# A selective scan of 64 states: every fourth state's input scaled on GpSimd token-major and turned by TensorE, one scan instruction a state

## The chip, the cores and the metric

The kernel runs on one core of one Trainium2 chip. The metric is the device time of one execution in microseconds; the kernel before takes 7624.67 us, the median of three runs (7620.87 to 7626.77). The engines are named as in the profile: PE is TensorE (PEld its weight loads), DVE is VectorE, ACT is ScalarE, POOL is GpSimd, SP is SyncE, which issues the DMAs.

## The reference

Four conditional layers follow one another on x of shape (16, 256, 256): an adapter, a bidirectional selective state-space layer with an MLP, and two transformer layers. Only the second layer's scan is touched, and it is where most instructions are. Cut to that:

```python
def _ssm(h, in_w, xproj_w, dt_bias, A_log, Dskip, out_w):   # h: (16, 256, 256)
    xz = h @ in_w
    xs, z = jnp.split(xz, 2, axis=-1)                        # 512 channels each
    xs = jax.nn.silu(xs)
    proj = xs @ xproj_w
    dt = jax.nn.softplus(proj[..., :D_INNER] + dt_bias)
    Bm = proj[..., D_INNER:D_INNER + D_STATE]                # 64 states
    Cm = proj[..., D_INNER + D_STATE:]
    A = -jnp.exp(A_log)
    def step(hst, ins):
        dt_t, B_t, C_t, x_t = ins
        dA = jnp.exp(dt_t[:, :, None] * A)
        hst = hst * dA + (dt_t * x_t)[:, :, None] * B_t[:, None, :]
        y_t = jnp.einsum('bds,bs->bd', hst, C_t)
        return (hst, y_t)
    ...                                                      # scan over 256 tokens
    y = jnp.swapaxes(ys, 0, 1) + xs * Dskip
    return y * jax.nn.silu(z) @ out_w
h_fwd = _ssm(h, ...)
h_bwd = jnp.flip(_ssm(jnp.flip(h, 1), ...), 1)
x = x + gate * (h_fwd + h_bwd)
```

## The kernel before

**Units and states.** A unit is one batch row in one direction: 16 x 2 = 32 units, each with 64 states; `steps` is the list of all 2048 (unit, state) pairs. For one state all 512 channels and 256 tokens are worked at once, channel-major: 128 partitions, four channel groups (`IC` = 4) of 256 tokens, 1024 elements a partition. A block below is eight consecutive states.

**What one state costs, in the order of the data.** `drive` (L931) makes the input on GpSimd: `dtx` (dt times x) times the state's row of B, which a DMA has spread over all partitions (`load_b`, four states at a time, SBUF tile `bb`). `decay` (L946) makes exp(dt x A) on ScalarE, four instructions a state, into PSUM. Three one-bank tiles `decays` take half a state (two channel groups) each in turn; column 0 of each group stays zero, so that one instruction can run through two groups without carrying a value over. `scan` (L974) runs two scans of 512 elements on VectorE, decay from PSUM, input from SBUF, result in place of the input in `h`; in the backward direction it walks the tokens from the end. Then `h` is multiplied by the state's row of C: for five states of eight on VectorE (L977), with C spread over the partitions by two TensorE transposes into the PSUM bank `cs` (`spread`, L961); for three of eight on GpSimd (L981), with C spread by a DMA (`load_c`, SBUF tile `cb`). `add_up` (L992) turns `h` by eight transposes that add into the PSUM tile `y`, which collects all 64 states.

**Order.** The main loop runs over k. In its turn k it emits the input of state k + 4 (`AHEAD`), the scan and C multiply of k, the decays of k + 1 and the sum of k - 2 (`BEHIND`), then one piece of the side work: `front` and `back` of the neighbouring units and `rest`, which is all other layers of a batch row. A scheduler orders each engine's instructions from this, by its own view of what is ready; GpSimd's multiplies are held in the order in which they are emitted (`keep_in_program_order`). Each engine works its queue in order. `h` tiles come from a ring of `NH` = 11. All DMAs are issued by SyncE, in one queue: `bb` and `cb` as well as the weights of all layers. Once a unit, `front` ends with four GpSimd multiplies of the same size (L452 to L461), the last of which makes `dtx`.

**PSUM.** Eight banks: three `decays`, one `cs`, two for `y`, two in `ps_g`, which the side work shares. After the last scan, the side work of the last batch row also takes the four banks of `decays` and `cs` (list `alone`).

Of the kernel before, what the change touches and what calls it, by code (L numbers as in the profile page):

```python
# [22 lines left out]
NS = 64  # L23
EPS = 1e-5


# [28 lines left out]
def kernel(ctx: ExitStack, tc: tile.TileContext, a: dict, out: bass.AP):  # L55
# [68 lines left out]
    SG = 4  # L124
    ND = 3
    NH = 11
    res = ctx.enter_context(tc.tile_pool(name="res", bufs=1))
# [6 lines left out]
    ps_y = ctx.enter_context(tc.tile_pool(name="ps_y", bufs=1, space=PSUM))  # L134
    ps_c = ctx.enter_context(tc.tile_pool(name="ps_c", bufs=1, space=PSUM))
    ps_g = ctx.enter_context(tc.tile_pool(name="ps_g", bufs=2, space=PSUM))
# [119 lines left out]
    for d in ("fwd", "bwd"):  # L256
        an = res.tile([P, IC, NS], F32, name=f"a_neg_{d}")
        nc.sync.dma_start(an, a[f"L1_cond_{d}_A_log"].rearrange("(c p) s -> p c s", p=P))
        nc.scalar.activation(an, an, AF.Exp)
        nc.vector.tensor_scalar(an, an, -1.0, None, ALU.mult)  # L260
        a_neg.append(an)
        w_bc.append(res.tile([P, IC, 2 * NS], F32, name=f"w_bc_{d}"))
        nc.sync.dma_start(w_bc[-1], chunked(a[f"L1_cond_{d}_xproj_w"])[:, :, DI:])
        w_out.append(res.tile([P, IC, D], F32, name=f"w_out_{d}"))
        nc.sync.dma_start(w_out[-1], chunked(a[f"L1_cond_{d}_out_w"]))


    decays = [ps_y.tile([P, 2, T], F32, name=f"decay{j}") for j in range(ND)]
    for dc in decays:
        nc.vector.memset(dc[:, :, 0:1], 0.0)  # L270

# [101 lines left out]
    def front(u):  # L373
# [13 lines left out]
        w_in, w_dt = wfront.pop(u)  # L387
        xz = s2.tile([P, 2 * IC, T], F32, name="xz")
        for m in range(0, 2 * IC, 2):
            px = halves(bank1("pxz"))  # L390
            for j in range(2):
                for c in range(DC):
                    nc.tensor.matmul(  # L393
                        px[:, j], w_in[:, c, (m + j) * P : (m + j + 1) * P], hT[:, c],
                        start=(c == 0), stop=(c == DC - 1),
                    )
                yield
            nc.scalar.copy(xz[:, m : m + 2], px)
        nc.scalar.activation(xz, xz, AF.Silu)
        exp_table()  # L400
        yield
        pb = bank1("pbc")
        for c in range(IC):
            nc.tensor.matmul(pb[:, :T], w_bc[d][:, c], xz[:, c], start=(c == 0), stop=(c == IC - 1))
        bc = s1.tile([P, T], F32, name="bc", tag="uu")
# [3 lines left out]
        yield  # L409
        pt = bank1("pct")  # L410
        for t in range(NT):
            nc.tensor.transpose(pt[:, t * P : (t + 1) * P], bc[:, t * P : (t + 1) * P], ident)
        cT = s2.tile([P, NT, NS], F32, name="cT")
        nc.scalar.copy(cT, pt[:, :T].rearrange("p (t s) -> p t s", t=NT)[:, :, NS:])
        yield


        pr = s1.tile([P, IC, T], F32, name="pr")
        for m in range(0, IC, 2):
            pp = halves(bank1("pdt"))  # L420
            for j in range(2):
                for c in range(IC):
                    nc.tensor.matmul(  # L423
                        pp[:, j], w_dt[:, c, (m + j) * P : (m + j + 1) * P], xz[:, c],
                        start=(c == 0), stop=(c == IC - 1),
                    )
                yield
            for j in range(2):
                nc.scalar.activation(  # L429
                    pr[:, m + j], pp[:, j], AF.Identity, bias=col(f"L1_cond_{name}_dt_bias", m + j)  # L430
                )
            yield
# [27 lines left out]
        yield  # L460
        tc.keep_in_program_order(nc.gpsimd.tensor_tensor(dtx, dt, xz[:, 0:IC], ALU.mult))  # L461
        st[u] = (xz, cT, bd, dt, dtx)
        yield

    def back(u, yg):
# [12 lines left out]
        for m in range(DC):  # L478
            xb = xs[b][:, m]
            nc.vector.scalar_tensor_tensor(  # L480
                xb, po[:, m], m_mamba[:, 4 + m, b : b + 1], xb, ALU.mult, ALU.add
            )
# [81 lines left out]
    def heads2(q, k, v, o, rows):  # L564

        exs, exTs = {}, {}
        for i in range(16 + 3):
# [30 lines left out]
            if i % 2 and i >= 3:  # L598
                yield
                po = bank2("po")[:, :T]  # L600
                for h in (i - 3, i - 2):
                    exT = exTs.pop(h)
                    base = (h % 2) * 64
                    for kt in range(NT):
                        nc.tensor.matmul(  # L605
                            po[base : base + 64], v[:, kt, h * 64 : (h + 1) * 64], exT[:, kt],
                            start=(kt == 0), stop=(kt == NT - 1),
                        )
# [55 lines left out]
    def heads3(q, k, v, oT):  # L664
# [28 lines left out]
        def values(g):  # L693
# [14 lines left out]
            po = bank2("po3")[:, :T]  # L708
            for j in range(4):
                for kt in range(NT):  # L710
                    nc.tensor.matmul(
# [180 lines left out]

    bbs, cbs, ys, made, hs, skips = {}, {}, {}, {}, {}, {}
    cs = ps_c.tile([P, 2, T], F32, name="cs")
    steps = [(u, s) for u in range(len(units)) for s in range(NS)]
    turn = [0]

    def load_b(u, g):
        bd = st[u][2]
        bb = s3.tile([P, SG, T], F32, name="bb")  # L900
        nc.sync.dma_start(bb, bd[g * SG : (g + 1) * SG, :].partition_broadcast(P))
        bbs[u, g] = bb

    def load_c(u, g):
        bd = st[u][2]
        cb = s3.tile([P, 3, T], F32, name="cb")
        nc.sync.dma_start(
            cb,
            bd[NS + 8 * g + 1 : NS + 8 * g + 8 : 3, :].partition_broadcast(P),
        )  # L910
        cbs[u, g] = cb

    def drive(k):
        u, s = steps[k]
        if s % SG == 0:
            if s == 0:
                load_b(u, 0)
            if s + SG < NS:
                load_b(u, s // SG + 1)
            if s % 8 == 0:  # L920
                load_c(u, s // 8)
        if s == 0:
# [4 lines left out]
            skips[u] = skip  # L927
        h = s3.tile([P, IC, T], F32, name="h", bufs=NH)
        bb = bbs[u, s // SG][:, s % SG]
        tc.keep_in_program_order(  # L930
            nc.gpsimd.tensor_tensor(h, st[u][4], bb.unsqueeze(1).to_broadcast([P, IC, T]), ALU.mult)  # L931
        )
        hs[k] = h

    def decay(k):
        u, s = steps[k]
        d = units[u][1]

        when = slice(1, T) if d == 0 else slice(T - 2, None, -1)
        made[k] = []  # L940
        for i in range(2):
            dc = decays[turn[0] % ND]
            turn[0] += 1
            for j in range(2):
                c = 2 * i + (j if d == 0 else 1 - j)
                nc.scalar.activation(  # L946
                    dc[:, j, 1:T], st[u][3][:, c, when], AF.Exp, scale=a_neg[d][:, c, s : s + 1]
                )
            made[k].append(dc)


    near = [k for k, (u, s) in enumerate(steps) if s % 8 in (0, 2, 3, 5, 6)]
    nth = {k: i for i, k in enumerate(near)}

    def spread(i):

        if i >= len(near):
            return
        u, s = steps[near[i]]
        for t in range(NT):  # L960
            nc.tensor.transpose(  # L961
                cs[:, i % 2, t * P : (t + 1) * P], st[u][1][:, t, s : s + 1].to_broadcast([P, P]), ident
            )

    def scan(k):
        u, s = steps[k]
        d = units[u][1]
        h = hs[k]
        for i, dc in enumerate(made.pop(k)):
            hv = h[:, 2 * i : 2 * i + 2].rearrange("p c t -> p (c t)")  # L970
            dv = dc.rearrange("p c t -> p (c t)")
            if d == 1:
                hv = hv[:, ::-1]
            nc.vector.tensor_tensor_scan(hv, dv, hv, 0.0, ALU.mult, ALU.add)  # L974
        if k in nth:
            c = cs[:, nth[k] % 2]
            nc.vector.tensor_tensor(h, h, c.unsqueeze(1).to_broadcast([P, IC, T]), ALU.mult)  # L977
        else:
            c = cbs[u, s // 8][:, (s % 8) // 3]
            tc.keep_in_program_order(  # L980
                nc.gpsimd.tensor_tensor(h, h, c.unsqueeze(1).to_broadcast([P, IC, T]), ALU.mult)  # L981
            )

    def add_up(k):
# [4 lines left out]
        for n, h in enumerate(([skips.pop(u)] if s == 0 else []) + [hs.pop(k)]):  # L989
            for t in range(NT):  # L990
                for c in range(IC):
# [5 lines left out]
                    )  # L997

# [138 lines left out]
    for k in range(AHEAD):  # L1139
        drive(k)  # L1140
    decay(0)
    spread(0)
    spread(1)
    other = late()
    for k in range(len(steps) + BEHIND):
        if k < len(steps):
# [6 lines left out]
            if k + 1 < len(steps):  # L1153
                decay(k + 1)
        if k >= BEHIND:
            add_up(k - BEHIND)
        if k - 1 in nth:
            spread(nth[k - 1] + 2)
        if k >= BEHIND:
            u, s = steps[k - BEHIND]  # L1160
            if s == NS - 1:
# [5 lines left out]
                for i in range(2):  # L1167
                    py = halves(bank1("py"))
                    for j in range(2):
# [3 lines left out]
                    nc.vector.tensor_tensor(  # L1173
                        yg[:, 2 * i : 2 * i + 2], py, st[u][0][:, IC + 2 * i : IC + 2 * i + 2], ALU.mult
                    )
# [6 lines left out]
    drain(other)  # L1182
    alone += [None] + [t.rearrange("p c t -> p (c t)") for t in (decays[0], cs, decays[1])]
    alone += [None, decays[2].rearrange("p c t -> p (c t)")]
    while waiting:
# [29 lines left out]
```

## Time and profile before

| | |
|---|---|
| median of three runs | 7624.67 us |
| span of the profiled execution | 7616.3 us |
| GpSimd input multiply, L931, x2048 | 4793.5 us busy, 2367 ns each |
| VectorE scan of 512, L974, x4096 | 4748.8 us busy, 1213 ns each |
| TensorE sums, L992, x16384 | 2385.3 us busy |
| ScalarE decays, L946, x8192 | 3641.4 us busy, 471 to 474 ns each |
| GpSimd C multiply, L981, x768 | 1813.2 us busy, 2361 ns each |
| VectorE C multiply, L977, x1280 | 1533.5 us busy, 1215 ns each |
| TensorE spreads of C, L961, x2560 | 521.6 us busy |
| DMA | 675.90 MB, mean 89 GB/s |

In the groups of instructions a line names the source line, engine and operation, then output and inputs with their partitions x elements and how many there are; after the first bar stand the busy time of the group and the mean of one in ns, after the second the time the engine sat idle just before them and what ended it. A wait line names who waited for whom, the total, how often and the longest. A timeline line has start, length, engine and instruction; neighbours of one kind are merged.

### The profile page before, as it was taken

The numbers are of one execution on the slowest core, as the hardware profiler recorded it, in microseconds if no ns is written. First come the engines' busy times: TensorE is split into PE (matmuls) and PEld (weight loads), VectorE is DVE, ScalarE is ACT, GpSimd is POOL, SyncE is SP. The second block draws the span as 40 slices with busy tenths as digits, with TensorE's granted clock in tenths as the row PEclk, the third lists the DMA queues.
The fourth block names the chain that finished last, engine by engine and source line by source line (L and its number), as shares of the span: only waits on it lengthen the run. The fifth ranks groups of instructions, "written<-read, shape, count | busy, mean of one in ns | idle before, by whom it ended". The sixth has DMA issues, their size and how long they took to land.

```text
span 7616.3 us, 100847 instructions
## 1 busy us (share of the span) xinstructions
PE 6249.2 (82%) x35471; PEld 4952.4 (65%) x35471; DVE 6860.6 (90%) x6887; ACT 5431.2 (71%) x12141; POOL 6843.8 (90%) x2959
## 2 busy tenths in 40 slices
PE   7568888888888888888888888888888888888778
PEld 4456676666667666676666666666666766666655
DVE  3988999999999999999999999999999999999982
ACT  4567777777777777777777777777777777777753
POOL 3999999999999999999999999999999999999960
PEclk8679999999999999999999999999999999999999
DMA  4112232222322222232222223222232222322221
GB/s 166 54 65 92 89 102 76 87 92 88 103 85 93 80 91 95 92 103 73 88 92 91 100 86 98 78 92 93 87 106 79 94 84 89 101 91 89 73 68 49
DMA packets 331644, 675.90 MB, mean 89 GB/s; under 512 B 24724, under 2 KB 204032, under 8 KB 326784
## 3 DMA queue, kind: packets, MB, share of 16 engines
q1 hardware_dynamic: 331136, 669.44, 26.7%
q8 instruction: 280, 4.59, 0.2%
q14 instruction: 228, 1.87, 0.1%
HBM read 650.22 MB, written 10.75 MB: 87 GB/s over the span
## 4 chain that ended last, share of the span: by engine, by line
DVE 47%; POOL 15%; issue 14%; ACT 12%; PE 10%; DVEq 0%; POOLq 0%; ACTq 0%
DVE h L974 34%; POOL h L931 8%; DVE h L977 8%; ACT decay L946 5%; POOL h L981 5%; PE y L992 3%; DVE maxima L682 1%; ACT L155 1%; PE dense L500 1%; PE down L511 1%; PE bank L108 1%; PE po L605 1%; POOL uu L452 1%; POOL dt L458 1%; POOL dtx L461 1%
## 5 line engine op out<-in xcount | busy, mean ns | idle before, releaser
L974 DVE TENSOR_TENSOR_SCAN h<-decay,h 128x512 f32<-128x512 f32 x4096 | 4748.8, 1213 | 283.1 <-ACT decay L946 196.6
L931 POOL TENSOR_TENSOR h<-dtx,bb 128x1024 f32<-128x1024 f32 x2048 | 4793.5, 2367 | 129.2 <-PE y L992 128.4
L992 PE MATMUL y<-ident,h 128*128 128x128 f32 x16384 | 2385.3, 292 | 693.0 <-POOL h L981 639.1
L992 PEld LDWEIGHTS y<-ident,h 128*128 128x128 f32 x16384 | 2054.6, 151 | 1047.6 <-POOL h L981 733.1
L946 ACT ACTIVATE decay<-dt,a_neg_bwd 128x255 f32<-128x255 f32 x4096 | 1816.8, 471 | 759.9 <-DVE h L974 718.3
L946 ACT ACTIVATE decay<-dt,a_neg_fwd 128x255 f32<-128x255 f32 x4096 | 1824.6, 474 | 613.0 <-DVE h L974 571.6
L981 POOL TENSOR_TENSOR h<-h,cb 128x1024 f32<-128x1024 f32 x768 | 1813.2, 2361 | 289.8 <-DVE h L974 275.1
L977 DVE TENSOR_TENSOR h<-h,cs 128x1024 f32<-128x1024 f32 x1280 | 1533.5, 1215 | 66.2 <-PE cs L961 56.6
L961 PE MATMUL cs<-ident,cT 128*128 128x128 f32 x2560 | 521.6, 294 | 131.8 <-DVE h L977 130.3
L961 PEld LDWEIGHTS cs<-ident,cT 128*128 128x128 f32 x2560 | 331.4, 147 | 216.0 <-DVE h L977 192.0
L572 PE MATMUL sc<-k,q 64*128 64x256 f32 x960 | 293.4, 429 | 16.7 <-ACT ex L581 16.0
L393 PE MATMUL pxz<-hTm,w_in 128*128 128x256 f32 x1024 | 267.6, 388 | 15.9 <-DVE maxima L682 12.1
L679 PE MATMUL sc<-kd,qk 128*128 128x512 f32 x490 | 251.4, 614 | 33.5 <-DVE maxima L682 20.8
L700 PE MATMUL scT<-qk,kd 128*128 128x256 f32 x984 | 251.1, 386 | 28.7 <-DVE qk L691 23.2
L581 ACT ACTIVATE ex<-sc,nmax 128x256 f32<-128x256 f32 x480 | 222.7, 468 | 71.2 <-DVE nmax L577 68.5
L423 PE MATMUL pdt<-xz,w_dt 128*128 128x256 f32 x1024 | 247.3, 385 | 0.0
L572 PEld LDWEIGHTS sc<-k,q 64*128 64x128 f32 x960 | 172.6, 200 | 105.3 <-issue 34.2
L393 PEld LDWEIGHTS pxz<-hTm,w_in 128*128 128x128 f32 x1024 | 181.4, 194 | 53.1 <-DVE maxima L682 15.5
L700 PEld LDWEIGHTS scT<-qk,kd 128*128 128x128 f32 x984 | 175.5, 190 | 60.7 <-ACT pr L429 25.0
L577 DVE TENSOR_REDUCE nmax<-sc 128x2 f32<-128x512 f32 x240 | 163.9, 683 | 49.5 <-PE sc L572 48.8
L423 PEld LDWEIGHTS pdt<-xz,w_dt 128*128 128x128 f32 x1024 | 190.7, 194 | 22.2
L595 ACT COPY exT<-pt 128x512 f32<-128x512 f32 x240 | 140.0, 583 | 86.2 <-PE pt L591 84.0
(350 smaller groups left out, 7571.4 us busy)
## 6 DMA issues: line engine op xcount, KB each, us to landing
bb<-bd SPq DMA_DIRECT2D x512, 512.0 KB
cb<-bd SPq DMA_DIRECT2D x256, 384.0 KB
l2w<-in_L_cond_W_dram SPq DMA_DIRECT2D x32, 1024.0 KB
l3w<-in_L_cond_W_dram SPq DMA_DIRECT2D x32, 1024.0 KB
l1w<-in_L_cond_mlp_w_dram SPq DMA_DIRECT2D x48, 512.0 KB
w_in<-in_L_cond_fwd_in_w_dram SPq DMA_DIRECT2D x16, 1024.0 KB
w_dt<-_L_cond_fwd_xproj_w_dram SPq DMA_DIRECT2D x16, 1024.0 KB
w_in<-in_L_cond_bwd_in_w_dram SPq DMA_DIRECT2D x16, 1024.0 KB
```

The lines of the kernel that those rows point to most:

```text
L393: nc.tensor.matmul(px[:, j], w_in[:, c, (m + j) * P : (m + j + 1) * P], hT[:, c], start=(c == 0), stop=(c == DC - 1),)
L423: nc.tensor.matmul(pp[:, j], w_dt[:, c, (m + j) * P : (m + j + 1) * P], xz[:, c], start=(c == 0), stop=(c == IC - 1),)
L572: nc.tensor.matmul(sc[:, t], q[base : base + 64, ch, t * P : (t + 1) * P], k[base : base + 64, ch], start=True, stop=True,)
L679: nc.tensor.matmul(sc, q[:, g, t * P : (t + 1) * P], kd[g % 2][:, 2 * i : 2 * i + 2], start=True, stop=True)
L700: nc.tensor.matmul(sc[:, kt], kd[g % 2][:, j, kt * P : (kt + 1) * P], q[:, g], start=True, stop=True)
L931: nc.gpsimd.tensor_tensor(h, st[u][4], bb.unsqueeze(1).to_broadcast([P, IC, T]), ALU.mult)
L946: nc.scalar.activation(dc[:, j, 1:T], st[u][3][:, c, when], AF.Exp, scale=a_neg[d][:, c, s : s + 1])
L961: nc.tensor.transpose(cs[:, i % 2, t * P : (t + 1) * P], st[u][1][:, t, s : s + 1].to_broadcast([P, P]), ident)
L974: nc.vector.tensor_tensor_scan(hv, dv, hv, 0.0, ALU.mult, ALU.add)
L977: nc.vector.tensor_tensor(h, h, c.unsqueeze(1).to_broadcast([P, IC, T]), ALU.mult)
L981: nc.gpsimd.tensor_tensor(h, h, c.unsqueeze(1).to_broadcast([P, IC, T]), ALU.mult)
L992: nc.tensor.matmul(ys[u][:, t, c * P : (c + 1) * P], h[:, c, t * P : (t + 1) * P], ident, start=(s == 0 and n == 0 and c == 0), stop=(s == ...
```

## The change

For three states of four the input is made as before. For every fourth (s % 4 = 3) `dtx` is kept in a second, token-major copy `xT`, made once a unit by `turn` (eight transposes, two ScalarE copies); there B is one value a partition, so GpSimd scales `xT` by a column of `bT` (`scale`, two instructions of 128x512), and `put_in` turns the result by eight transposes into PSUM. Its decays go to an `h` tile in SBUF.

The three half-state banks and `cs` become two slots of two banks, each with a whole state, so each state has one scan of 1024 elements; `dt` at the first token is set to 1e34 after `dtx` is made, and A is at most -1e-30, so that the first decay of each channel group is 0. States with s % 8 in 0, 2, 4 scan into `h` and are multiplied by C on GpSimd; the other five scan in place in their slot, and VectorE multiplies from there into `h`. C comes by DMA for all states, four at a time, and B for three of four. The backward direction is stored reversed by `front`, so that all scans run forward. `h` has 9 tiles. `xz` is split into `xv` and `zv`. In `heads2` and `heads3` the loops around the matmuls of `po` change places.

```diff
-    SG, ND, NH = 4, 3, 11
+    SG, NH = 4, 9
...
-    decays = [ps_y.tile([P, 2, T], F32, name=f"decay{j}") for j in range(ND)]
+    slots = [ps_y.tile([P, IC, T], F32, name=f"slot{j}") for j in range(2)]
...
+            to = (xv, zv)[m // IC][:, m % IC : m % IC + 2]
+            nc.scalar.copy(to, px[:, :, ::-1] if d else px)
...
+        tc.keep_in_program_order(nc.gpsimd.memset(dt[:, :, 0:1], APART))
...
+    def turn(u):
+        xT = s1.tile([P, NT, DI], F32, name="xT")
+        for t in range(NT):
+            pt = bank1("pxt")
+            for c in range(IC):
+                nc.tensor.transpose(pt[:, c * P : (c + 1) * P], st[u][4][:, c, t * P : (t + 1) * P], ident)
+            nc.scalar.copy(xT[:, t], pt)
+        xTs[u] = xT
...
-        cb = s3.tile([P, 3, T], F32, name="cb")
+        cb = s3.tile([P, SG, T], F32, name="cb")
+        nc.sync.dma_start(cb, bd[NS + g * SG : NS + (g + 1) * SG, :].partition_broadcast(P))
...
     def drive(k):
...
+        if s % SG < SG - 1:
             h = s3.tile([P, IC, T], F32, name="h", bufs=NH)
...
     def decay(k):
+        if s % SG < SG - 1:
+            dc = slots[s % 2]
+        else:
+            dc = hs[k] = s3.tile([P, IC, T], F32, name="h", bufs=NH)
+        for c in range(IC):
+            nc.scalar.activation(dc[:, c], st[u][3][:, c], AF.Exp, scale=a_neg[d][:, c, s : s + 1])
+
+    def scale(k):
+        u, s = steps[k]
+        sx = s2.tile([P, NT, DI], F32, name="sx")
+        for t in range(NT):
+            tc.keep_in_program_order(
+                nc.gpsimd.tensor_scalar(
+                    sx[:, t], xTs[u][:, t], st[u][5][:, t, s : s + 1], 1.0, ALU.mult, ALU.mult
+                )
+            )
+        scaled[k] = sx
+
+    def put_in(k):
+        sx = scaled.pop(k)
+        for t in range(NT):
+            for c in range(IC):
+                nc.tensor.transpose(
+                    slots[1][:, c, t * P : (t + 1) * P], sx[:, t, c * P : (c + 1) * P], ident
+                )
+
+    def on_vector(s):
+        return s % 8 not in (0, 2, 4)
 
     def scan(k):
+        h, ps = hs[k], slots[s % 2]
+        c = cbs[u, s // SG][:, s % SG].unsqueeze(1).to_broadcast([P, IC, T])
+        if s % SG == SG - 1:
+            nc.vector.tensor_tensor_scan(flat(ps), flat(h), flat(ps), 0.0, ALU.mult, ALU.add)
+        else:
+            to = ps if on_vector(s) else h
+            nc.vector.tensor_tensor_scan(flat(to), flat(ps), flat(h), 0.0, ALU.mult, ALU.add)
+        if on_vector(s):
+            nc.vector.tensor_tensor(h, ps, c, ALU.mult)
+        else:
+            tc.keep_in_program_order(nc.gpsimd.tensor_tensor(h, h, c, ALU.mult))
...
     # main loop, turn k, after scan(k)
             if k + 1 < len(steps):
-                decay(k + 1)
+                if s % SG == SG - 2:
+                    put_in(k + 1)
+                else:
+                    decay(k + 1)
+                if s % SG == SG - 3:
+                    scale(k + 2)
+                    decay(k + 2)
+            if s == NS - 2 and k + 2 < len(steps):
+                turn(u + 1)
```

## The prediction

> **What bounds the kernel now.** I read the page's totals and chain first. A "block" is eight states below; 32 units of 64 states make 256 blocks.
>
> ```profile
> span 7616.3 us, 100847 instructions
> PE 6249.2 (82%) x35471; PEld 4952.4 (65%) x35471; DVE 6860.6 (90%) x6887; ACT 5431.2 (71%) x12141; POOL 6843.8 (90%) x2959
> DVE 47%; POOL 15%; issue 14%; ACT 12%; PE 10%; DVEq 0%; POOLq 0%; ACTq 0%
> ```
>
> Two engines are at 90%, and the chain changes between them: a shared bound. The span lies 8.4 us under the median of the runs (7624.67); I sum against the span and add 8.4. The pace comes from an instruction that runs once a unit:
>
> ```profile
> L461 POOL TENSOR_TENSOR dtx<-dt,xz x32: 2338/2362/2397, 134.7 to 7072.3; 128x1024 f32<-128x1024 f32 x32
> ```
>
> (7072.3 - 134.7)/31 = 223.8 us a unit, **27.97 us a block**. Then the groups of the stretch from 440 to 7360 us (247.4 blocks), without head and tail:
>
> ```profile
> L974 DVE TENSOR_TENSOR_SCAN h<-decay,h 128x512 f32<-128x512 f32 x3912 | 4535.9, 1213 | 264.4 <-ACT decay L946 188.5 <-POOL h L931 70.2 <-ACT low L352 3.6
> L977 DVE TENSOR_TENSOR h<-h,cs 128x1024 f32<-128x1024 f32 x1222 | 1463.5, 1216 | 54.8 <-PE cs L961 45.7 <-DVE h L974 0.5
> L931 POOL TENSOR_TENSOR h<-dtx,bb 128x1024 f32<-128x1024 f32 x1956 | 4579.1, 2367 | 129.1 <-PE y L992 128.4
> L981 POOL TENSOR_TENSOR h<-h,cb 128x1024 f32<-128x1024 f32 x734 | 1733.4, 2362 | 264.2 <-DVE h L974 254.7 <-issue 5.1 <-POOL h L931 3.8
> ```
>
> VectorE is busy 6487.8 us there (26.2 a block: scans 18.3, C multiplies 5.9, the other layers 2.0). GpSimd has these two groups and four multiplies a unit of 2.36 us: 6596 us, 26.7 a block. So GpSimd has 1.3 us a block to spare and VectorE 1.75. Next, the timeline of VectorE where little beside the scan runs, for the pitch of its instructions:
>
> ```profile
> 225.39 1.20 DVE L977 TENSOR_TENSOR h<-h,cs 128x1024 f32<-128x1024 f32 x1
> 226.50 2.33 DVE L974 TENSOR_TENSOR_SCAN h<-decay,h 128x512 f32<-128x512 f32 x2
> 228.75 1.20 DVE L977 TENSOR_TENSOR h<-h,cs 128x1024 f32<-128x1024 f32 x1
> 229.86 4.56 DVE L974 TENSOR_TENSOR_SCAN h<-decay,h 128x512 f32<-128x512 f32 x4
> 234.33 1.20 DVE L977 TENSOR_TENSOR h<-h,cs 128x1024 f32<-128x1024 f32 x1
> ```
>
> Four scans take 4.47 us from start to start, 1.12 each, 0.1 less than the 1.213 that one lasts: neighbours overlap at their ends. GpSimd's likewise come every 2.31 us (six of L931 in 13.89). Last, the waits:
>
> ```profile
> PE y L992 <- POOL h L981: 639.1, 255, 8.3
> POOL h L981 <- DVE h L974: 275.1, 206, 7.4
> DVE h L974 <- ACT decay L946: 196.6, 199, 3.2
> POOL h L931 <- PE y L992: 128.4, 87, 5.8
> DVE h L974 <- POOL h L931: 80.7, 50, 5.9
> DVE h L977 <- PE cs L961: 56.6, 57, 3.5
> ```
>
> GpSimd waits for scans more than scans wait for GpSimd, and TensorE's queue stands behind states whose C multiply is on GpSimd.
>
> **The change, part by part (us a block).**
>
> *One scan a state.* An elementwise instruction of 1024 takes 1.216, one of 512 (L103) 0.683: 1.04 ns an element and 0.15 fixed. A scan of 512 at 1.213 is then 0.15 + 512 x 2.07 ns, one of 1024 2.27, at a pitch of 2.18. Eight cost 17.4 where sixteen cost 17.9. Bounds: 1.21 if the scan's price were by instruction, 2.43 if by element alone. In five of eight the result goes to PSUM in place, which no row of VectorE shows; ScalarE's in-place PSUM instruction (L113, 256 elements, 352 ns) is no dearer than its 370 ns copy of 256 out of PSUM (L609), so I add nothing. VectorE: 17.4 + 5 x 1.13 + 2.0 = **25.1**, from 25.5 by the same pitches.
>
> *Inputs of every fourth state.* GpSimd loses two multiplies of 2.31 and gets four scalings of 128x512, which no row shows. The nearest:
>
> ```profile
> L1127 POOL MEMSET kd<- 128x1024 f32 x2 | 1.8, 954 | 85.0 <-DMA wvpd<-wvp 85.0
> L64 POOL MEMSET onesm<- 128x128 f32 x1 | 0.2, 203 | 0.0
> masks.py:199 POOL TENSOR_SCALAR_AFFINE_SELECT ident<-ident 128x128 f32<-128x128 f32 x1 | 0.3, 290 | 0.0
> ```
>
> Write only: 0.84 ns an element, 0.10 fixed, so 0.53 at 512. One read with compare and select: 0.10 + 512 x 1.5 ns = 0.87. Half a two-input multiply: 1.18. A scaling has one read and no select: I take **0.65**, and keep 0.53 and 1.18 for the range. GpSimd: 9 x 2.31 + 4 x 0.65 + 1.16 (the four multiplies a unit) = **24.6**, from 26.6. The memset of four columns adds about 0.1 a unit.
>
> The Trainium skill (GPSIMD Engine Reference, § 3.1) puts a body of at most two ALU operations at 1.03 cycles an element, about 0.54 here as an estimate; no run here shows it, and the sum below would be 0.2 lower.
>
> *Turning them.* Sixteen transposes a block come, ten of L961 go, and 8 a unit come in `turn`: seven more a block. Eight of L992 take 1.04 in the timeline, so 0.9 of TensorE a block, hidden under its 18% idle; with that cover gone the gain is gone. They wait for GpSimd in TensorE's queue, and the y sums and the other layers' matmuls stand behind them; the C transposes of L961 no longer do.
>
> The Trainium skill (TensorE: Matmul & The Clock Gate, Part 4) speaks against this step: about 275 ns for a bf16 transpose in a kernel, 2.2 for eight as an estimate. The trace differs, 1.04 for eight, and decides; by the page the sum below would be 0.7 higher.
>
> *Slots.* Three half-state banks become two whole-state pairs. The exponentials of state s + 2 start when state s leaves its pair, for five of eight after the C multiply. For s = 1 and 5 only a 2.18 scan lies between, against four exponentials at 0.44 = 1.8 and two handovers of 0.1: 0.2 of slack, where a bank today has two scans (2.2) for two exponentials (0.9). ScalarE's work is unchanged (a fourth of it goes to SBUF: 496 ns by L926 for 472) but for two copies of 0.58 a unit. Today's waits for it are 188.5/247.4 = 0.76; I keep 0.76, because part falls into the slack of A below.
>
> *C by DMA.* SyncE issues 512 loads of 512 KB for 256 of 384, and the 512 loads of B shrink to 384 KB: 96 MB more, 14 GB/s on 89. A C load stands behind a B load in SyncE's queue and is issued four states ahead, some 13 us; at the mean 89 GB/s it lands in 6. Cost nothing; if it were late, states s = 0 and 4 would wait on GpSimd.
>
> *The order of matmuls in `po`, `NH` 9 for 11, reversed copies.* On engines with idle time: nothing. Nine buffers hold four ahead, the running one and two unsummed, less the fourth state's, so one or two spare; the 128.4 us wait for them is the bound of a loss, and part of my range.
>
> **The sum: a loop.** GpSimd's order is fixed: C0, input 5, scale 3, input 6, C2, input 8, C4, input 9, scale 7, input 10. From the end of scan 0:
> - A, to scan 3. VectorE: scan, multiply, scan, a quarter of the other layers: 2.18 + 1.13 + 2.18 + 0.5 = 6.0. GpSimd: C0 2.31, input 2.31, two scalings 1.3, the last four transposes 0.6, three handovers 0.3 = **6.8**, which decides.
> - B, scan 3, multiply, scan 4: 5.5 + 0.5 = 6.0.
> - C, to scan 7: VectorE 2 x 3.31 + 0.5 = **7.1** over GpSimd's 6.8.
> - D, scan 7, multiply, scan 0: 6.0.
>
> Sum 25.9; and 0.76 for ScalarE and 0.4 for the unit's four multiplies where they fall into A or C: **27.1** against 27.97. 0.87 x 256 = 223; 7616.3 - 223 + 8.4 = 7402; `turn(0)` ahead of the first scan (eight transposes, two copies) adds some 2 once, and I say **7400**. What GpSimd loses is mostly not cashed: VectorE, with 25.1 of its own, is late next.
>
> **Rivals.**
> 1. *The loop does not bite* (scaling at 0.53, waits absorbed): VectorE's 25.1 plus 1.1 of waits, 26.2, 7170. For it: with GpSimd 2 us shorter, the 70.2 on L931 and 45.7 on L961 can go. Against: A is above VectorE's need at any price over 0.25.
> 2. *The scaling is dear* (slower): place, `scale` between C0 and scan 3. At 1.18, A and C are 7.9 each, 27.7 with B and D, and 28.9 with the same additions: 7616 + 0.9 x 256 = 7850. It decides from 0.94 a scaling. For it: every two-input row is at 2.3 ns an element. Against: one input less.
> 3. *ScalarE's lockstep eats it.* Two slots leave 0.2 of slack twice a block, and other ScalarE work (7 us a block, 5431 less the 3641 of L946 over 256; a GELU of 1.91 with two table loads of 1.28 is 4.5) falls between. If 0.76 becomes 1.6, nothing is gained: 7620; if 2.0, 7720. Against: the later of each pair hides in A.
>
> **How the numbers follow.** Forecast 0.50 (26.4 to 27.8, so 7220 to 7580); rival 1 0.16; rival 2 0.16; rival 3 0.18 (0.05 within 0.2%, 0.11 slower, 0.02 faster). A measurement of this kernel can tell about 0.2%. Faster: nearly all of 0.50, 0.16 and 0.02, 0.66; same 0.06; slower 0.28. The range takes in most of rival 1 and the mild half of rival 3: 7130 to 7690.
>
> **What would show it.** Right: scans at 2.2 to 2.3 us; scalings at 0.6 to 0.7; VectorE waiting at the scan of every fourth state for TensorE's turned inputs, behind GpSimd; GpSimd's share below VectorE's. Wrong: scalings near 1.2 with GpSimd still at 90%; ScalarE's exponentials ending VectorE's waits at over 1.6 a block; scans in PSUM above 2.4. The forecast fails most easily on the scaling's price: 0.1 of it moves A by 0.2, 51 us in all.

## The result and the profile after

The changed kernel takes **8514.8 us** (median of four, 8510.0 to 8515.36) against 7623.38 for the kernel before beside it (four runs, 7620.87 to 7626.77): ratio **1.1165**, 95% interval 1.115 to 1.1181. The prediction was 7400, range 7130 to 7690, so even the sign was wrong.

The page of the profile after gives the span and each engine's busy time, and the view of the tile `dt` the last multiply of each unit's preparation (shortest/median/longest in ns, first and last start in us):

```profile
span 8512.7 us, 104750 instructions
...
PE 6639.1 (78%) x37263; PEld 5258.5 (62%) x37263; DVE 6874.0 (81%) x4836; ACT 5536.3 (65%) x12299; POOL 6352.3 (75%) x3503
```

```profile
L461 POOL TENSOR_TENSOR dtx<-dt,xv x32: 2329/2368/2405, 130.6 to 7902.5; 128x1024 f32<-128x1024 f32 x32
```

From the first to the last are 31 units: 250.7 us a unit, **31.34 us a block** of eight states, where the forecast had 27.1 and the kernel before 27.97. That is 3.37 x 256 = 863 of the 896 us by which the span grew. VectorE's work is the same (6874.0 us busy, 6860.6 before), GpSimd's is 491 us less. VectorE's idle time, span less busy, went from 755.7 to 1638.7. So the two busiest engines got no more work; they wait. The clock granted to TensorE, 0.916 against 0.932, doesn't explain it: of the runs below, `e11_half_plain` has 0.903 and takes 7794 us, `e17_nh10` has 0.928 and takes 8097. Five of the groups of instructions show the prices:

```profile
L982 DVE TENSOR_TENSOR_SCAN slot<-slot,h 128x1024 f32<-128x1024 f32 x768 | 1754.7, 2289 | 337.1 <-ACT slot L947 294.4 <-issue 36.7 <-POOL h L935 1.3
L982 DVE TENSOR_TENSOR_SCAN h<-slot,h 128x1024 f32<-128x1024 f32 x768 | 1752.8, 2282 | 464.6 <-ACT slot L947 454.5 <-POOL h L935 8.8
L984 DVE TENSOR_TENSOR h<-slot,cb 128x1024 f32<-128x1024 f32 x1280 | 1548.0, 1217 | 26.0 <-DMA cb<-bd 0.6
L979 DVE TENSOR_TENSOR_SCAN slot<-h,slot 128x1024 f32<-128x1024 f32 x512 | 1168.2, 2282 | 249.0 <-PE slot L964 237.5
L954 POOL TENSOR_SCALAR sx<-xT,bT 128x512 f32<-128x512 f32 x1024 | 697.3, 695 | 0.0
```

A scan of 1024 takes 2.28 to 2.29 us (2.27 forecast), in place in PSUM at most 7 ns more; a scaling 0.695 (0.65). The second half of the lines has the loss: VectorE stands ahead of its scans until ScalarE, or for every fourth state TensorE, has refilled the slot. Nine of the waits, with their totals, counts and longest:

```profile
ACT slot L947 <- DVE h L982: 1002.3, 545, 7.5
POOL h L986 <- DVE h L982: 845.7, 232, 15.3
ACT slot L947 <- DVE h L984: 760.4, 412, 14.9
PE slot L964 <- DVE h L984: 531.6, 242, 5.6
DVE h L982 <- ACT slot L947: 454.5, 253, 41.4
POOL h L935 <- PE y L996: 418.8, 193, 7.3
DVE slot L982 <- ACT slot L947: 294.4, 209, 5.9
DVE slot L979 <- PE slot L964: 237.5, 136, 8.4
POOL h L986 <- DMA cb<-bd: 137.6, 83, 4.5
```

Both directions are there: ScalarE waits 1763 us for VectorE to leave a slot, and VectorE 749 for ScalarE to fill one, 2.93 a block where 0.76 was kept (2.75 in the stretch from 500 to 8250 us, without head and tail; the expectations below use that figure). TensorE too waits for VectorE to leave a slot, 532 us, and only 43 for GpSimd's scaling there. A stretch without other trouble shows how; first VectorE's timeline, then ScalarE's:

```profile
5215.06 2.27 DVE L979 TENSOR_TENSOR_SCAN slot<-h,slot 128x1024 f32<-128x1024 f32 x1
5217.37 1.22 DVE L984 TENSOR_TENSOR h<-slot,cb 128x1024 f32<-128x1024 f32 x1
5218.51 2.28 DVE L982 TENSOR_TENSOR_SCAN h<-slot,h 128x1024 f32<-128x1024 f32 x1
5221.61 2.30 DVE L982 TENSOR_TENSOR_SCAN slot<-slot,h 128x1024 f32<-128x1024 f32 x1 [0.83 <-ACT slot L947]
```

```profile
5218.63 0.48 ACT L947 ACTIVATE slot<-dt,a_neg_fwd 128x256 f32<-128x256 f32 x1 [0.87 <-DVE h L984]
5219.04 0.49 ACT L947 ACTIVATE h<-dt,a_neg_fwd 128x256 f32<-128x256 f32 x1
5219.44 0.46 ACT L947 ACTIVATE slot<-dt,a_neg_fwd 128x256 f32<-128x256 f32 x1
5219.84 0.49 ACT L947 ACTIVATE h<-dt,a_neg_fwd 128x256 f32<-128x256 f32 x1
5220.24 0.46 ACT L947 ACTIVATE slot<-dt,a_neg_fwd 128x256 f32<-128x256 f32 x1
5220.64 0.57 ACT L1172 COPY yt<-y 128x512 f32<-128x512 f32 x1
5221.11 0.47 ACT L947 ACTIVATE slot<-dt,a_neg_fwd 128x256 f32<-128x256 f32 x1
```

The C multiply ends at 5218.59 and frees slot 1. One scan of 2.28 covers the refill. The four exponentials would need some 1.8 back to back, but the fourth state's decays (into `h`) and a copy stand between them in ScalarE's queue: 2.95 us from the first to the last, and VectorE waits 0.83. Over the whole trace, taking the slot exponentials four by four, from the start of the first to the end of the last, a fill lasts 2.58 us in the median and 2.95 in the mean; 66% of 1536 last longer than 2.2.

### The profile page after: what moved, and what is told of

Read it like the earlier page. It is cut to its first block, busy times and chain, and to the rows that moved or that the text cites. A ratio compares the mean times of both kernels' runs of the same rounds, so it can differ in the third digit from the quotient of the medians.

```text
span 8512.7 us, 104750 instructions
## 1 busy us (share of the span) xinstructions
PE 6639.1 (78%) x37263; PEld 5258.5 (62%) x37263; DVE 6874.0 (81%) x4836; ACT 5536.3 (65%) x12299; POOL 6352.3 (75%) x3503
## 5 line engine op out<-in xcount | busy, mean ns | idle before, releaser
L935 POOL TENSOR_TENSOR h<-dtx,bb 128x1024 f32<-128x1024 f32 x1536 | 3619.7, 2361 | 750.8 <-PE y L996 418.8
L982 DVE TENSOR_TENSOR_SCAN h<-slot,h 128x1024 f32<-128x1024 f32 x768 | 1752.8, 2282 | 464.6 <-ACT slot L947 454.5
L947 ACT ACTIVATE slot<-dt,a_neg_bwd 128x256 f32<-128x256 f32 x3072 | 1410.2, 471 | 976.9 <-DVE h L982 571.7
L982 DVE TENSOR_TENSOR_SCAN slot<-slot,h 128x1024 f32<-128x1024 f32 x768 | 1754.7, 2289 | 337.1 <-ACT slot L947 294.4
L947 ACT ACTIVATE slot<-dt,a_neg_fwd 128x256 f32<-128x256 f32 x3072 | 1403.4, 471 | 859.2 <-DVE h L982 430.6
L984 DVE TENSOR_TENSOR h<-slot,cb 128x1024 f32<-128x1024 f32 x1280 | 1548.0, 1217 | 26.0 <-DMA cb<-bd 0.6
L979 DVE TENSOR_TENSOR_SCAN slot<-h,slot 128x1024 f32<-128x1024 f32 x512 | 1168.2, 2282 | 249.0 <-PE slot L964 237.5
L964 PE MATMUL slot<-ident,sx 128*128 128x128 f32 x4096 | 671.1, 313 | 590.9 <-DVE h L984 531.6
L964 PEld LDWEIGHTS slot<-ident,sx 128*128 128x128 f32 x4096 | 547.4, 161 | 763.5 <-issue 402.3
L954 POOL TENSOR_SCALAR sx<-xT,bT 128x512 f32<-128x512 f32 x1024 | 697.3, 695 | 0.0
```

What stands on the lines that cost most here:

```text
L947: nc.scalar.activation(dc[:, c], st[u][3][:, c], AF.Exp, scale=a_neg[d][:, c, s : s + 1])
L954: nc.gpsimd.tensor_scalar(sx[:, t], xTs[u][:, t], st[u][5][:, t, s : s + 1], 1.0, ALU.mult, ALU.mult)
L964: nc.tensor.transpose(slots[1][:, c, t * P : (t + 1) * P], sx[:, t, c * P : (c + 1) * P], ident)
L979: nc.vector.tensor_tensor_scan(flat(ps), flat(h), flat(ps), 0.0, ALU.mult, ALU.add)
L982: nc.vector.tensor_tensor_scan(flat(to), flat(ps), flat(h), 0.0, ALU.mult, ALU.add)
L984: nc.vector.tensor_tensor(h, ps, c, ALU.mult)
```

## The experiments

Each is one execution beside one of the kernel before (7615 to 7629), unless an interval is given; differences under some 0.5% are not read. The names of theories are those of the expectations: 'order' is the order that the scheduler gives VectorE, 'chain' the path C multiply, input, scaling, transposes and scan of the fourth state, 'slots' the slot of a whole state as the unit that is handed over, 'release' its hold over the C multiply, 'rings' the buffers of `h` and `cb`.

**First four: each suspect by itself.**

`e1_pin`. VectorE's order in the changed kernel isn't that of the states: scans are put ahead of C multiplies, and state 4's scan ahead of state 3's in 216 of the 256 blocks. Here both are held to the order of the states.

```diff
-            nc.vector.tensor_tensor(h, ps, c, ALU.mult)
+            held(nc.vector.tensor_tensor(h, ps, c, ALU.mult))      # behind the one emitted before; the scans too
```

> Only the order on VectorE is changed: scans and C multiplies stand by state, each multiply right behind its own scan (in the kernel after, the scan of the next state often stands ahead of the multiply, so a slot comes free a scan later). Theory 'order': VectorE's waits for ScalarE's exponentials fall from 2.75 us a block of eight states to about 1, the block from 31.3 to 28 us, the run to 7600 to 7800 us. Theory 'chain' (GpSimd's scaling and TensorE's transposes feed every fourth state too late): no gain, 8400 to 8700, since no later scan may pass the fourth state. Theory 'slots' (two whole-state slots are too few in any order): 8200 to 8500.

Measured 8612.08, in the range of 'chain'. VectorE's waits for ScalarE's slots fell to 404 us, but GpSimd's wait at its C multiply rose from 846 to 1673. The scheduler's order is not the cause; it helps.

`e2_plain`. The token-major part is undone: all inputs by GpSimd multiplies, all decays into slots.

```diff
-        if s % SG < SG - 1:
-            dc = slots[s % 2]
-        else:
-            dc = hs[k] = s3.tile([P, IC, T], F32, name="h", bufs=NH)
+        dc = slots[s % 2]
```

> Every state's input is a GpSimd multiply again and its decay goes to a slot; slots, one scan a state and C by DMA stay. 'chain': the cause is gone, GpSimd's 26.6 us a block sets the pace, 27.5 to 28.5, the run 7550 to 7800 us. 'slots' and 'order': still 30 to 32 a block, 8200 to 8600, with VectorE waiting for ScalarE.

Measured 8472.13, in the range of 'slots' and 'order'. With whole slots, undoing the part that gives the change its name takes back no more than 43 us of the 891, with 486 us more of GpSimd's work in it. VectorE still waits 765 us for ScalarE at its scans, and a fill still lasts 2.50 us in the median, though ScalarE's queue holds no decays for `h` here.

`e3_noscale`. The transposes of every fourth state read `xT` unscaled; B is left out for these states and GpSimd has 683 us less to do.

```diff
-        sx = scaled.pop(k)
+        sx = xTs[steps[k][0]]
```

> TensorE turns the unscaled copy for every fourth state: the multiplication by B is left out there, and 2.8 us a block of GpSimd with it; the transposes and their place stay. 'chain': GpSimd no longer stands before them, the block falls to 28 to 29, the run to 7700 to 7900. 'slots' and 'order': VectorE still waits 2 us or more a block for ScalarE, 8200 to 8500.

Measured 8529.82, far from the range of 'chain' and just above that of 'slots' and 'order': GpSimd's time isn't the bound, and the scaling's price isn't the cause.

`e4_oneexp`. One exponential of 1024 for four of 256, with the A of the first channel group for all.

```diff
-        for c in range(IC):
-            nc.scalar.activation(dc[:, c], st[u][3][:, c], AF.Exp, scale=a_neg[d][:, c, s : s + 1])
+        nc.scalar.activation(dc, st[u][3], AF.Exp, scale=a_neg[d][:, 0, s : s + 1])
```

> The four exponentials of a state become one instruction over all four channel groups (with the A of the first group): filling a slot takes about 1.07 us for 1.8. 'slots' and 'order': a slot is filled 0.7 sooner wherever VectorE waits for it, the waits for ScalarE fall from 2.75 to about 1, the block to 28 to 29, the run to 7700 to 8000. 'chain': below 1% of gain, 8430 or more.

Measured 8566.75, though ScalarE is busy 4347 us instead of 5536 and a fill is one instruction of 1.12 us. By the expectation this speaks for 'chain', which `e2_plain` speaks against, and against 'slots' as a mere price of the refill: a faster refill by ScalarE alone gains nothing. VectorE's waits for ScalarE's slots fell from 749 to 271, and others came in their place:

```profile
POOL h L935 <- PE y L995: 1273.7, 306, 12.0
...
DVE slot L978 <- PE slot L963: 510.7, 193, 9.7
```

The engine that a wait names is the one that was last and need not be the cause: with one filled faster, VectorE stands for the next one. Whole slots are handed round ScalarE, TensorE and VectorE, and `h` round GpSimd, VectorE and TensorE.

**Second four: the unit that is handed over.**

`e7_toh`. All scans write to `h`, so that a slot is free when its scan ends.

```diff
-            to = ps if on_vector(s) else h
+            to = h
-            nc.vector.tensor_tensor(h, ps, c, ALU.mult)
+            nc.vector.tensor_tensor(h, h, c, ALU.mult)
```

> The changed kernel with every scan's result in h, none in place in its slot; the C multiply of VectorE reads h and C from SBUF. The slot is then free when the scan ends, not 1.2 us later after the C multiply. Theory 'release' (the slot held over the C multiply is what makes VectorE wait for the refill, 2.75 us a block): those waits fall to 1.0 or less and the time to 7700 to 8050. Theory 'rings' (C loads issued late because cb has two buffers, and nine h buffers): both rings stay, so the time stays within 1.5% of 8515. Theory 'slots' (a slot of a whole state refilled only when the whole scan is done): a third to a half of the 892 us goes, 8050 to 8250. A price that it adds: if VectorE's multiply with all three operands in SBUF keeps GpSimd off, the mean of either engine's multiplies rises above 1.22 and 2.36 us.

Measured 9257.57, far outside. The price that the last sentence names decides; groups of this kernel:

```profile
L935 POOL TENSOR_TENSOR h<-dtx,bb 128x1024 f32<-128x1024 f32 x1536 | 4020.6, 2623 | 298.2 <-issue 185.1 <-PE y L996 112.1 <-ACT v L777 1.1
L984 DVE TENSOR_TENSOR h<-h,cb 128x1024 f32<-128x1024 f32 x1280 | 2522.7, 1980 | 18.5
L954 POOL TENSOR_SCALAR sx<-xT,bT 128x512 f32<-128x512 f32 x1024 | 1038.8, 1025 | 0.0
```

VectorE's multiply went from 1217 to 1980 ns, GpSimd's from 2361 to 2623, its scaling from 695 to 1025. VectorE's waits for ScalarE's slots are still 652 us, though a slot is free a C multiply earlier; that speaks against 'release', but with these prices around it the run is no clean test. It does say that the multiply's operand has to stay in PSUM here.

`e8_plain_rings`. `e2_plain`, with the room that this frees given to `NH = 10` and three `cb`.

> The changed kernel with the input of every fourth state a GpSimd multiply again (as in e2_plain, 8472), and with the room that this frees given to the rings: three cb buffers for two, ten h for nine. Theory 'rings': GpSimd's waits for C loads (312.9 us in e2_plain) and for h buffers (510.8) fall below 150 each, and the time to 7750 to 8000. Theories 'release' and 'slots': these waits shrink but VectorE's wait for the slots stays at 600 to 1000 us and the time above 8300.

Measured 8372.55, 100 us less than `e2_plain`. The wait for C loads is gone, VectorE's 765 us for ScalarE remain. GpSimd's wait for `h` fell only from 511 to 418 us, so the ring of `h` was not fully eased; what was eased holds a ninth of the loss.

`e10_half`. Half-state slots, with all else of the change left in.

```diff
-    slots = [ps_y.tile([P, IC, T], F32, name=f"slot{j}") for j in range(2)]
+    slots = [[ps_y.tile([P, 2, T], F32, name=f"slot{j}{i}") for i in range(2)] for j in range(2)]
...
+        for i, ps in enumerate(slots[s % 2]):          # two scans of 512, then two C multiplies of 512
```

> The changed kernel with two scans and two C multiplies a state again, each on a half-state slot of its own (four of one bank for two of two), so that ScalarE or TensorE can refill the first half while the second is scanned. All else of the change stays. Prices: eight more scan instructions and five more multiplies a block, 0.05 to 0.1 us each by pitch, so about +1 us a block, +250 us, if nothing is gained. Theory 'slots': the waits for refills fall by over half and the time to 7900 to 8200. Theory 'release': half of the hold goes, 8200 to 8400. Theory 'rings': 8500 to 8750.

Measured **8062.69**, 452 us less than the changed kernel, in spite of 95 us more work on VectorE (6968.9). VectorE's waits for ScalarE's slots are these three, 266 us for 749 (the columns as above):

```profile
DVE h L985 <- ACT slot L948: 94.6, 103, 4.1
DVE slot L985 <- ACT slot L948: 86.9, 103, 1.2
DVE slot L982 <- ACT slot L948: 84.9, 70, 2.4
```

A half slot is filled in 0.99 us in the median, and 7% of the fills last over 2.2. What is left stands elsewhere: TensorE waits 511 us for GpSimd's scaling at the slot, where it waited 43 with whole slots.

`e11_half_plain`. `e8_plain_rings` with half slots.

> e8_plain_rings with half-state slots: plain inputs, three cb and ten h buffers, and two scans a state. What is left of the change is C by DMA, the C multiply out of the slot, and four half slots for three. Theory 'slots' together with 'rings': 7600 to 7850, near the kernel before. Theory 'release' alone: above 8100, since the slots are still held over the C multiply.

Measured 7793.68, in the range of the two theories together: 579 less than with whole slots, the largest gain of a single edit in all runs. VectorE's waits for ScalarE's slots are now these two, 152 us for 765:

```profile
DVE h L979 <- ACT slot L945: 102.1, 54, 4.5
DVE slot L979 <- ACT slot L945: 49.5, 61, 3.7
```

**Third four: what half slots leave.**

`e12_half_early`. `e10_half` with the scaling emitted at the end of the group before. That is two turns of the loop earlier, ahead of three GpSimd multiplies (two inputs and a C multiply); the expectations say some three states.

```diff
-                    scale(k + 2)
...
+            if s % SG == SG - 1 and k + SG < len(steps):
+                scale(k + SG)
```

> e10_half (8063) with the scaling of the next fourth state moved from behind GpSimd's C multiply of the state before it to the end of the group before, some three states earlier. Theory 'chain' (with half slots, what is left of the loss is the path C multiply, input, scaling, transposes, scan of the fourth state): TensorE's wait at the slot for the scaled input, 511 us, falls below 150, VectorE's wait for the turned input (263.9) below 100, and the time to 7700 to 7900. Theory 'order' (VectorE's scheduler-made order keeps GpSimd's C multiplies waiting): no more than 100 us faster, 7950 to 8070.

Measured **7820.98**, another 242 less; TensorE's wait for the scaling at the slot is no longer among its larger ones. The time is in the range of 'chain', but VectorE's wait for the turned input is 220.6 us, not below 100: the open end below comes back to it. Two edits that keep the idea of the change have now taken back 694 of 891 us.

`e13_half_pin` and `e14_half_early_pin` hold VectorE's order, as `e1_pin` did, on `e10_half` and `e12_half_early`.

> e10_half with VectorE's scans and C multiplies held to the order of the states. Theory 'order': GpSimd's waits at its C multiply (853.7 us in all) halve, and the time falls to 7700 to 7900. Theory 'chain': VectorE now stands at every fourth state until the turned input is there; 8000 to 8300.

> Both of the two above on e10_half. If 'chain' and 'order' each hold a part, this is the fastest of the three: 7500 to 7700, VectorE above 90% of the span. If 'chain' holds it all, within 1% of e12_half_early. If it is slower than e12_half_early by over 1%, the scheduler's order was a help and not a cause.

Measured 8330.64 and 8093.08, 268 and 272 more than without. With `e1_pin` (97 more) that makes three of three: the order by readiness pays.

`e15_scan2`. Two scans of half a state, but the slot stays one tile and the C multiply one instruction.

> The changed kernel (8515) with two scans of half a state in each slot, but one C multiply of the whole state, as one instruction: the slots of the five states of eight with the multiply on VectorE come free as a whole, those of s = 0, 2, 4 by halves. Theory 'slots' as the wait for the scan's end: half or more of the 452 us that e10_half won, 8060 to 8290. Theory 'release' (the C multiply's hold counts): 8400 to 8600, since the hold is as long as before.

Measured 8505.64, no gain. That is in the range of 'release', but the expectation assumed that the halves would come free one by one, and ScalarE's timeline, and VectorE's after it, show that they don't, so the run can't tell 'slots' from 'release':

```profile
3023.31 1.50 ACT L947 ACTIVATE slot<-dt,a_neg_bwd 128x256 f32<-128x256 f32 x3 [0.73 <-DVE h L984]
```

```profile
3019.78 1.21 DVE L984 TENSOR_TENSOR_SCAN h<-slot,h 128x512 f32<-128x512 f32 x1
...
3022.02 1.20 DVE L984 TENSOR_TENSOR_SCAN h<-slot,h 128x512 f32<-128x512 f32 x1
```

The first half was scanned by 3020.99, yet ScalarE starts at 3023.31, 0.09 after the second half: the slot is released as a whole tile. So `e10_half`'s gain comes from the smaller unit that is handed over, not from shorter scan instructions. How it divides between the scan's and the C multiply's hold, no run shows.

**Last six: whether the two causes add up, and the last 192 us.**

`e16_whole_early`. The edit of `e12_half_early` on the changed kernel.

> The changed kernel (8515, whole-state slots, one scan a state) with only the scaling moved ahead by some three states, as in e12_half_early. If the two causes add up, 8250 to 8330 (242 us less, or a little under). If the slots' refill is the bound and the late scaling hides behind it, 8420 to 8530. If the scaling's chain was the larger cause all along, below 8100.

Measured 8425.42, at the lower end of the second case. The two edits make a table of four (us):

| | scaling as changed | scaling two turns earlier |
|---|---|---|
| slots of a whole state | 8515 | 8425 |
| slots of half a state | 8063 | 7821 |

The earlier scaling is worth 90 behind whole slots and 242 behind half slots: part of the late scaling hides behind the refill. Not all of the 90 need be the path of the fourth state: in the changed kernel TensorE waits only 43 us for the scaling at the slot, while ScalarE, between units, waits 17 times to overwrite the one buffer of `xT` until the last scaling has read it, 111 us in all; here that is 8. How the 90 divides, no run shows.

`e17_nh10`, built on `e12_half_early`, and on it `e18_c45` and `e19_c4`, which move C multiplies to GpSimd.

```diff
-    NH = 9
+    NH = 10
-        sx = s2.tile([P, NT, DI], F32, name="sx")
+        sx = s2.tile([P, NT, DI], F32, name="sx", bufs=1)
...
-        return s % 8 not in (0, 2, 4)
+        return s % 8 not in (0, 2, 4) and s % 16 != 6      # e18_c45; s % 2 == 1 in e19_c4
```

> e12_half_early (7821) with one buffer for the scaled input instead of two and the 4 KB a partition that this frees given to a tenth h buffer. Theory 'h ring': GpSimd's wait for h (372.1 us behind TensorE's y sums) falls below 200 and the time to 7650 to 7760. Theory 'VectorE's load': the wait falls, the time stays, 7780 to 7850.

> e17_nh10 with one C multiply in 16 states moved from VectorE to GpSimd (s = 6 of every second block): VectorE 6950 - 128 x 1.29 = 6785 us busy, GpSimd 6348 + 128 x 2.36 = 6650. Theory 'VectorE's load': 120 to 200 us faster than e17_nh10. Theory 'h ring' alone: within 60 us of it. A version that beats the kernel before (7624) would show here or in the next.

> e17_nh10 with one C multiply in 8 states moved to GpSimd, so that all even states have theirs there: VectorE 6620 us busy, GpSimd 6950. GpSimd is now the fuller engine: 7500 to 7750 if it reaches the 90% that it had in the kernel before; slower than e18_c45 if its waits for VectorE's scans (0.6 to 0.9 ms) stay as they are.

Measured 8097.33, 8045.04 and 8105.00. GpSimd's wait for `h` went to nothing, as 'h ring' said, and the time rose by 276, since the buffer taken from `sx` made a new wait in GpSimd's queue, the first of its list:

```profile
POOL sx L955 <- PE slot L965: 925.6, 171, 13.3
```

`e18_c45` gained 52 us, below the 120 of 'VectorE's load', and `e19_c4` lost 60 again; both have the new wait too (866 and 780 us). So these three don't judge the ring.

`e20_early_c45` is `e12_half_early` with the C multiplies of `e18_c45`; `e21_ahead3` has `AHEAD, BEHIND = 3, 2` besides.

> e12_half_early (7821; nine h and two sx buffers) with one C multiply in 16 states moved from VectorE to GpSimd, as between e17_nh10 and e18_c45, where it took 52 us off. Theory 'VectorE's load' (90 us more busy than the kernel before, by half multiplies): 7640 to 7740. Theory 'h ring': within 60 us of 7821, and GpSimd's wait for h stays at 300 us or more. By e18 as a scale: 7770.

> e20_early_c45 with the inputs made three states ahead instead of four, so that one h buffer more is free at any time; B and C loads are issued one state later too. Theory 'h ring': GpSimd's wait for h behind TensorE's y sums falls by half or more and the time 80 to 200 us below e20_early_c45, perhaps below the kernel before (7624). Theory 'VectorE's load': within 60 us of e20_early_c45. If C loads or inputs are now late: slower, with GpSimd or VectorE waiting for cb, or VectorE's scans for GpSimd.

Measured 7871.08 (ratio to the kernel before 1.0321, 1.0303 to 1.0338) and 7899.90 (1.036, 1.0344 to 1.0375). VectorE has 131 us less to do than in `e12_half_early`, GpSimd some 290 more, and the time is 50 more: 'VectorE's load' by itself falls as the cause of the rest. Making inputs three states ahead left GpSimd's wait for `h` at 466 us (468 in `e20_early_c45`), so the ring wasn't eased by it, and its part stays open. No version here beats the kernel before; `e11_half_plain`, 2.2% slower, comes nearest.

## Why the prediction was wrong

**The step that failed is "Slots".** It set "four exponentials at 0.44 = 1.8 and two handovers of 0.1" against a scan of 2.18, found 0.2 of slack, and kept 0.76 us a block for ScalarE. The trace after has fills of 2.58 in the median, and VectorE's waits for ScalarE at 2.93 a block. The exponentials were no dearer than assumed (0.40 from start to start in the stretch above); what was wrong was to take four in a row. ScalarE's queue also holds the copies and table loads of the side work, which are enough by themselves (`e2_plain`), and the fourth state's decays, which the same change had moved there. That is rival 3's mechanism, which the prediction put at 0.18 and priced at up to 2.0 a block, 7720; "over 1.6 a block" was also its own sign of being wrong. By its own scale of 256 us for 1 us a block, 2.93 makes 7620 + 1.33 x 256 = 7960, so half of the miss is still not in it.

**What else the sum had too low.** In the stretch from 500 to 8250 us the 31.34 a block are 26.3 of VectorE's work, 2.75 of waits for ScalarE's slots, 0.83 for TensorE's turned inputs and 1.5 of other waits. The turned inputs cost what the forecast had, the 0.8 by which GpSimd's path exceeds VectorE's in A, but that is luck: TensorE stood at the slot for VectorE (532 us), not for GpSimd (43). VectorE's own 25.1 was 1.2 too low: it took the pitch of undisturbed neighbours, by which the kernel before has 25.5, where the working itself reads 26.2 of busy time for it. For all other waits the sum had 0.4. So of the 4.2 a block that were missed, ScalarE's slots are 2.0. This says where the time stands, not what each part is worth when it is taken out, as `e4_oneexp` shows.

**The step one level up.** The sum went through VectorE's scans in the order of the states, with each handover at 0.1, and looked for the slowest engine of each stretch. With a unit of a whole state and two of them, the waits show VectorE stopped by each partner in turn: ScalarE, TensorE's transposes (237.5 us), and in `e4_oneexp` GpSimd by way of `h`. Which one a wait names changes from run to run (`e1_pin`, `e4_oneexp`) while the time stays at 8567 to 8612; the size of the unit changes it by 452 to 579 (`e10_half`, `e11_half_plain`). And the loop's parts A and C, with the scaling behind the C multiply, were seen as a chain that the half slots lay bare, but taken as the bound of the kernel as it stands, where moving the scaling ahead gains 90 us.

**Right:** the scan of 1024 (2.27, measured 2.28 to 2.29) and its write into PSUM at no charge; the scaling (0.65, measured 0.695), so rival 2, which needs 0.94, falls; eight transposes in 1.04. The estimate of 0.54 for the scaling, worked out from the Trainium skill (GPSIMD Engine Reference, § 3.1), was lower than the 0.695 measured, and by either the time would be as far off.

**"C by DMA: cost nothing"** was nearly so: GpSimd waits 161 us for `cb`, on an engine that now idles 2160; three buffers instead of two, with a tenth `h`, gave 100. **"`NH` 9 for 11: nothing"**: GpSimd's wait for `h` rose from 128 to 419; what it costs by itself isn't shown.

**Rival 1** (the loop does not bite, 7170) falls with VectorE at 81%.

**Open:** the last 192 us of `e12_half_early` over the kernel before. 90 are VectorE's work (6950.4 against 6860.6, ten half multiplies of 0.676 for five of 1.215), but taking 131 of work away, at the price of more on GpSimd, didn't help. A place where VectorE waits 9 us in that kernel, first its own timeline, then TensorE's:

```profile
3015.33 2.34 DVE L982 TENSOR_TENSOR_SCAN slot<-h,slot 128x512 f32<-128x512 f32 x2 [8.95 <-PE slot L965]
```

```profile
3007.37 1.46 PE L423 MATMUL pdt<-xv,w_dt 128*128 128x256 f32 x6
3008.66 1.88 PE L773 MATMUL pv<-wv,hT 128*128 128x512 f32 x4
3010.38 1.04 PE L1000 MATMUL y<-ident,h 128*128 128x128 f32 x8
3011.25 3.60 PE L773 MATMUL pv<-wv,hT 128*128 128x512 f32 x8
3014.69 1.04 PE L965 MATMUL slot<-ident,sx 128*128 128x128 f32 x8
```

TensorE's 0.9 a block was to be hidden under its idle time; its time is (82% busy here), its place in the queue isn't. The turned input stands behind the matmuls of other layers; all such waits of VectorE come to 221 us there. `e11_half_plain`, which has no such transposes, is 171 over the kernel before all the same, so they aren't the whole of it. No run moved the transposes ahead of those matmuls, and no changed version had eleven `h` buffers again.

## What to carry to other kernels

When buffers between engines are made fewer and larger, price the refill by how long it lasts in the queue of the engine that does it, other work between its instructions included, and set that against what the consumer still has to do meanwhile; the sum of the instructions' durations was only the lower bound here (1.8 against 2.58). When engine loads stay as they were and the time rises, try a smaller unit of hand-over before hunting the engine that the waits name: here that engine changed from run to run. A buffer taken from one ring for another turned up as a wait of the first (`e17_nh10`).

## What the runs showed of the hardware

VectorE's multiply with all operands in SBUF, in `e7_toh`, took 1980 ns where the same with one operand in PSUM takes 1217, and lengthened GpSimd's instructions beside it (2361 to 2623, 695 to 1025). The Trainium skill (SBUF — State Buffer, section "SBUF: two separate sides") states that a VectorE instruction with two SBUF inputs and a GpSimd instruction that reads SBUF lock a shared port pair for the whole instruction, the other being blocked; these rows agree with it, on both sides. The split by overlap does too: in `e7_toh` VectorE's multiplies that overlap a GpSimd multiply or scaling take 2112 ns in the mean, the others 1215; GpSimd's input multiplies that overlap one of VectorE's take 2754, the others 2355. In the changed kernel, with one operand in PSUM, VectorE's take 1217 either way. A scan in place in PSUM took 2289 ns where the decay was in the slot and 2282 where the input was; one into SBUF took 2282.
